# An LSTM scan with a residual: x @ Wx by Strassen products over pairs of steps, one tanh for three gates, and new orders

## The chip, the cores and the metric

One core of a Trainium2 chip. The metric is device time in microseconds of one execution. The kernel before took 2259.08 us, the median of three runs (2258.97 to 2259.52).

## The reference

Input x has 16 sequences of 512 steps with 512 features; h0 is 16 x 512, Wx and Wh are 512 x 2048, b has 2048 entries. All are float32.

```python
xW = jnp.einsum('ntd,dg->ntg', x, Wx) + b
def step(carry, xw_t):
    prev_h, prev_c = carry
    a = xw_t + prev_h @ Wh
    i = sigmoid(a[:, :H]); f = sigmoid(a[:, H:2*H])
    o = sigmoid(a[:, 2*H:3*H]); g = tanh(a[:, 3*H:])
    next_c = f * prev_c + i * g
    next_h = o * tanh(next_c)
    return (next_h, next_c), next_h
_, hs = scan(step, (h0, zeros), swapaxes(xW, 0, 1))
out = x + swapaxes(hs, 0, 1)
```

Each step needs the h of the one before, so h @ Wh and the gates form a chain of 512 links. x @ Wx does not depend on h and can be done at any time ahead.

## The kernel before, in words

**Layout.** A step has only 16 rows. TensorE's array is used as four column groups: matmuls with 32 stationary columns and j = 0..3 write to partitions 32j of one PSUM bank, four of them side by side. 32 columns are 16 rows of two steps (a pair, for x) or 16 rows of two parts of a number (for h). The 512 hidden units lie as 4 (chunk c) x 4 (j) x 32 (u). The hidden units fall into halves a and b (h = 0, 1: chunks 0, 1 and chunks 2, 3); each half has its own PSUM banks `gates[h]`, two for even and odd steps.

**h @ Wh in 16 bits.** Wh is split once into three float16 matrices wq[0..2], and each step's h into float16 parts: p1 (the leading part), p2 (the rest against a stored multiple of h, `hist`) and p2r (a reflected rest by way of `rem`). `products(t, i, kh, h)` (L237) adds one combination: matrix i, rows from half kh, result half h; it is eight matmuls of 256 columns, in four column groups. Matrix 3 needs p1 alone, matrix 1 needs p2 too, matrix 2 needs p2r. In half b, matrix 3 and matrix 2 read a second copy of p1 in another slot, in half a matrix 2 does. The copy is made by ScalarE (L340).

**A step** t is emitted as the list STEP_PE for TensorE, and STEP for VectorE (DVE) and ScalarE (ACT); every engine takes its own instructions strictly in the order in which they are emitted, waiting on semaphores. STEP_PE is twelve products, named by matrix and halves (q3aa: matrix 3, from a to a), then x0 and x1: two chunks of x @ Wx for a pair two ahead (`project`, L214, float32, 512 columns; a float32 matmul runs as two instructions, so x0 and x1 are 16 rows of the trace). The result lands in one of four PSUM banks xb, which already hold the bias (`put_bias`, L198, ACT).

STEP turns finished gates into the next h, for a and b interleaved:

- turn and turno (L272, DVE): transposes from PSUM, of g, i, f (192 columns) and of o (64);
- fold and foldo (L279, DVE): join high and low parts, in float32;
- tanh, sig, sigo (L306, L308, L312, ACT): tanh of g, sigmoid of i and f, sigmoid of o; scale (L314, ACT): o times a power of two;
- mix (L316, DVE): i g and f c in one product; cell (L322, DVE): their sum, the new c; ctanh (L324, ACT);
- p1 (L336, DVE), h (L330, DVE, writes `hist`), copy (L340, ACT), p2 (L342), rem (L346), p2r (L350), all DVE.

After STEP come the two seeds of step t + 2 (L224, ACT: they copy x @ Wx of the step from xb into the gate banks, masked by step parity), and in alternate steps either the bias of a coming pair and a residual, or the scaling of a finished pair back to h (`unscale`, L361, ACT) and the transpose of a coming x (`turn_x`, L210, DVE). A residual transposes the scaled pair (hb, L387, DVE), adds x (L388, GpSimd) and stores it: blocks of 16 steps by 32 DMAs (L368), in the last block pair by pair, 8 DMAs each (L377), all on the queue of SyncE (SP). x comes in blocks of 16 steps on the same queue (L177), two blocks ahead, issued in the first step of a block. The last two rows are stored by `last_sum` (L403), partly from ACT's queue.

The start (L538 to L562) scales and splits Wh, does h0 @ Wh (`first_products`, L249), the first x blocks and step 0, in an order written out by hand (START).

Of the kernel before, what the change touches and what calls it, by code (L numbers as in the profile page):

```python
# [22 lines left out]
STEP_PE = "q3aa q3ab q1ab q1aa q2aa q3ba q1ba q2ba q2bb q1bb q2ab q3bb x0 x1"  # L23
STEP = (
    "turn_a turno_a fold_a tanh_a foldo_a sig_a turn_b sigo_a scale_a mix_a fold_b "
    "tanh_b cell_a ctanh_a turno_b foldo_b sig_b p1_a sigo_b h_a copy_a mix_b p2_a "
    "scale_b cell_b rem_a ctanh_b p2r_a p1_b h_b copy_b p2_b rem_b p2r_b"
# [3 lines left out]
    "turn_a turno_a fold_a turn_b foldo_a tanh_a fold_b sig_a turno_b sigo_a foldo_b "  # L31
    "tanh_b mix_a sig_b cell_a sigo_b ctanh_a mix_b cell_b ctanh_b h_a h_b"
)

# [8 lines left out]
    "d2.2 fold_b tanh_a foldo_a sig_a foldo_b r2.6 d3.2 tanh_b sigo_a sigo_b sig_b "  # L46
    "P.1.3 q3.2.s mix_a mix_b P.2.0 cell_a cell_b r2.5 scale_a ctanh_a ctanh_b scale_b "
    "P.2.1 seed.1.0 seed.1.1 p1_a h_a h_b copy_a p1_b q3.5.s p2_a rem_a rem_b p2r_a "
    "q3.6.v copy_b p2_b p2r_b seed.2.0 seed.2.1"
# [4 lines left out]
def lstm_residual(ctx: ExitStack, tc: tile.TileContext, x, h0, wx, wh, b, out):  # L54
# [82 lines left out]
    sc = const.tile([P, 2, 4], FP, tag="sc", name="sc")  # L137
    neg = const.tile([P, P], FP, tag="neg", name="neg")
    neg16 = const.tile([P, P], HP, tag="neg16", name="neg16")
    rows = [const.tile([P, P], FP, tag=f"rows{h}", name=f"rows{h}") for h in range(2)]  # L140
    S, RS, RS2, RSL = ([sc[:, h, i : i + 1] for h in range(2)] for i in range(4))
# [5 lines left out]
    AT = (((1, 3, 0), (0, 3, 1)), ((0, 3, 2), (0, 2, 3)))  # L147
    SLOTS = (((1, 2, 3, 4), (1, 0, 4, 3)), ((0, 1, 3, 4), (1, 0, 3, 2)))
# [3 lines left out]
        [const.tile([P, 2, 5 * N], HP, tag=f"parts{h}{i}", name=f"parts{h}{i}") for i in range(2)]  # L152
# [42 lines left out]
    xT = {}  # L195
# [4 lines left out]
    def turn_x(q):  # L200
        s, i = divmod(q, XP)
        if i == 0 or q <= FIRST:

            a, e = (i, i + 1 if q < FIRST else XP)
            seen = tmp.tile([P, XP, NK], FP, tag="seen", name=f"seen_{q}")
            nc.vector.tensor_copy(
                seen[:, a:e], xs[s].rearrange("p i (c u) -> p i c u", c=NK)[:, a:e, :, 0]
            )
        xT[q] = xtp.tile([P, NK, Q], FP, tag="xT", name=f"xT_{q}")
        nc.vector.transpose(xT[q].rearrange("p c m -> p (c m)"), xs[s][:, i])  # L210

    def project(q, c):
        for j in range(NJ):
            nc.tensor.matmul(  # L214
                xb[q % NXB][j * Q : (j + 1) * Q],
                lhsT=xT[q][:, c],
                rhs=wx_j[:, c, j],
                start=False,
                stop=False,
                skip_group_check=True,  # L220
            )

    def seed(t, h):
        nc.scalar.mul(  # L224
            gates[h][t % 2][:, :GU].rearrange("p (g u) -> p g u", g=G),
            xb[t // 2 % NXB].rearrange("p (g h u) -> p h g u", g=G, h=2)[:, h],
            mask[:, t % 2 : t % 2 + 1],
        )


    def products(t, i, kh, h):
        g = gates[h][t % 2]
        a = parts[kh][t % 2]
        k = AT[kh][t % 2][i - 1]
        for cc in range(2):
            for j in range(NJ):
                nc.tensor.matmul(  # L237
                    g[j * Q : (j + 1) * Q, :GU],
                    lhsT=a[:, cc, k * N : (k + 2) * N],
                    rhs=wq_j[i - 1][:, 2 * kh + cc, h, j],  # L240
                    start=False,
                    stop=False,
                    skip_group_check=True,
                )

    def first_products(c):
        for e in range(2):
            for j in range(NJ):
                nc.tensor.matmul(  # L249
                    xb[0][j * Q : (j + 1) * Q, (1 - e) * GU : (2 - e) * GU],  # L250
                    lhsT=hT0[:, c],
                    rhs=wh_j[:, c, e, j],
                    start=False,
                    stop=False,
                    skip_group_check=True,
                )


    gc = [state.tile([P, 2, 2 * N], FP, tag=f"gc{h}", name=f"gc{h}_init") for h in range(2)]
# [28 lines left out]
    def slots(t, h, kind):  # L288

        k = SLOTS[h][(t + 1) % 2][kind]  # L290
        return parts[h][(t + 1) % 2][:, :, k * N : (k + 1) * N]
# [4 lines left out]
    def act(t, op, h):  # L296
# [8 lines left out]
        elif op == "tanh":  # L305
            nc.scalar.activation(gc[h][:, 0], v["pre", h][:, 0], AF.Tanh)  # L306
        elif op == "sig":
            nc.scalar.activation(  # L308
                new("sif", t, h, [P, 2, 2 * N]), v["pre", h][:, 1:3], AF.Sigmoid
            )  # L310
# [4 lines left out]
        elif op == "mix":  # L315
            nc.vector.tensor_tensor(  # L316
                new("pr", t, h, [P, 2, 2 * N]), v["sif", h], gc[h], ALU.mult
            )
        elif op == "cell":
            gc[h] = state.tile([P, 2, 2 * N], FP, tag=f"gc{h}", name=f"gc{h}_{t}")  # L320
            pr = v["pr", h]
            nc.vector.tensor_tensor(gc[h][:, 1], pr[:, 0], pr[:, 1], ALU.add)  # L322
        elif op == "ctanh":
            nc.scalar.activation(new("tch", t, h, [P, 2 * N]), gc[h][:, 1], AF.Tanh)  # L324
# [10 lines left out]
        elif op == "p1":  # L335
            nc.vector.tensor_tensor(  # L336
                slots(t, h, 0), two(v["os", h]), two(v["tch", h]), ALU.mult
            )
        elif op == "copy":
            nc.scalar.copy(slots(t, h, 2), slots(t, h, 0))  # L340
        elif op == "p2":
            nc.vector.scalar_tensor_tensor(  # L342
                slots(t, h, 1), slots(t, h, 0), -LO, hl(t, h), ALU.mult, ALU.add
            )
        elif op == "rem":
            nc.vector.scalar_tensor_tensor(  # L346
                new("rem", t, h, [P, 2, N]), slots(t, h, 0), -LO, hl(t, h), ALU.mult, ALU.add
            )
        else:
            nc.vector.scalar_tensor_tensor(  # L350
                slots(t, h, 3), v["rem", h], 2.0, slots(t, h, 1), ALU.mult, ALU.subtract
            )
# [4 lines left out]
    def unscale(p, h):  # L357
        if h == 0:
            hs[p] = work.tile([P, NK, Q], FP, tag="hs", name=f"hs_{p}")
        a = slice(2 * h, 2 * h + 2)  # L360
        nc.scalar.mul(hs[p][:, a], hist[p // XP][:, p % XP, a], RSL[h])  # L361
# [20 lines left out]
    def residual(p):  # L382
# [3 lines left out]
        hb = work.tile([P, P], FP, tag="hb", name=f"hb_{p}")  # L386
        nc.vector.transpose(hb, hs[p].rearrange("p c m -> p (c m)"))  # L387
        nc.gpsimd.tensor_tensor(ob[s][:, i], hb, xs[s][:, i], ALU.add)  # L388
        if s == NS - 1:
            put_pair(s, i)  # L390
        elif i == XP - 1:
# [18 lines left out]
    hT0 = work.tile([P, NK, Q], FP, tag="hT0", name="hT0", bufs=1)  # L410
    warm = const.tile([1, 1], FP, tag="warm", name="warm")
    brow = const.tile([1, G * H], FP, tag="brow", name="brow")
    ones = const.tile([1, Q], FP, tag="ones", name="ones")
    nc.scalar.dma_start(out=brow, in_=b.rearrange("(o f) -> o f", o=1))
# [7 lines left out]
    nc.vector.memset(ones, 1.0)  # L422
    nc.gpsimd.memset(neg, 0.0)
# [45 lines left out]
    for bank in xb:  # L469
        for e in range(2):  # L470
            for j in range(NJ):
                nc.tensor.matmul(  # L472
                    bank[j * Q : (j + 1) * Q, (1 - e) * GU : (2 - e) * GU],
                    lhsT=ones,
                    rhs=brow.rearrange("p (e g c j u) -> p e j g c u", e=2, g=2, c=NK, j=NJ)[
                        :, e, j
                    ],
# [23 lines left out]
    def scales(h):  # L501
# [15 lines left out]
        nc.vector.tensor_scalar(rows[h], neg, RS[h], -1.0, ALU.mult, ALU.mult)  # L517
# [11 lines left out]
    def split(op, n, on_act):  # L529

        c, e = divmod(n, 2)
        w = wh_sb[:, c, e * GH : (e + 1) * GH]
        f = [q[:, c, (1 - e) * GH : (2 - e) * GH] for q in wq]
        if op[0] == "d":
            i = int(op[1])
            for m in range(2):
# [3 lines left out]
                    lhsT=rows[c // 2] if i == 1 else neg16,  # L540
# [8 lines left out]
        elif op == "q2" and n in BY_PE:  # L549
            nc.vector.scalar_tensor_tensor(f[1], w, RS[c // 2], f[0], ALU.mult, ALU.subtract)  # L550
        elif op == "q1":
            cast(on_act, f[0], w, RS2[c // 2])
        elif op == "r1":
            r1[n] = tmp.tile([P, GH], FP, tag="r1", name=f"r1_{n}", bufs=4)
            nc.vector.scalar_tensor_tensor(
                r1[n], w, RS[c // 2], f[0], ALU.mult, ALU.subtract
# [9 lines left out]
    def start(op, a="", b=""):  # L566
# [4 lines left out]
        elif op == "hT":  # L571
            nc.vector.transpose(hT0.rearrange("p c m -> p (c m)"), h_in)
        elif op == "xT":
# [17 lines left out]

    for t in range(1, T):
        s, ti = divmod(t, XB)
        q, half = divmod(t + 4, 2)
        if ti == 0:
            hist[s] = outp.tile([P, XP, NK, Q], FP, tag="hist", name=f"hist_{s}")

        for op in STEP_PE.split():
            if op[0] == "x":
                if q < NP:  # L600
                    project(q, 2 * half + int(op[1:]))
            else:
                products(t, int(op[1]), "ab".index(op[2]), "ab".index(op[3]))
# [4 lines left out]

        if t == T - 3:
            for h in range(2):  # L610
                unscale(t // 2, h)
            residual(t // 2)
        if t + 2 < T:
            seed(t + 2, 0)
        if t == T - 2:
# [5 lines left out]
        elif t % 2 == 0:  # L621
            if q + 1 < NP:
                put_bias(q + 1)
            residual(t // 2 - 1)
        elif t < T - 3:
            for h in range(2):
                unscale(t // 2, h)
            if q + 1 < NP:
                turn_x(q + 1)
        if t + 2 < T:  # L630
            seed(t + 2, 1)
        if ti == 0 and s + 2 < NS:
# [29 lines left out]
```

## Time and profile before

| | |
|---|---|
| median of the runs shown | 2259.08 us |
| span of the profiled execution | 2257.4 us |
| median less span | 1.7 us |
| granted TensorE clock, mean | 0.999 |
| products, start to start, steps 3 to 508 | 4.337 us a step |
| last products (step 511) start | 2248.18 us |
| last DMA issue starts | 2254.6 us |

The profiled execution's own device time is not listed apart from its span; its span is set beside the median. How to read it: the share of busy time is a mean over the run, but from about 45 us to 2235 us the run is one step repeated, so the timeline of a few steps says all about it. A timeline row gives start, duration, engine, line and operation, the tile written and those read, and in brackets the idle time before it with what released it. Neighbouring instructions of one kind are merged, and the end of a group of matmuls is modelled; starts are the better numbers. PE is TensorE's matmuls, PEld its weight loads, which can run ahead. Times within a step, in what follows, count from the start of its first x matmul where nothing else is said.

### The profile page before, as it was taken

How to read it: one execution, taken by the hardware profiler on the slowest of the kernel's cores; microseconds unless marked ns; L12 is line 12 of the kernel's file. 1: busy time of each engine (PE TensorE's matmuls, PEld its weight loads, DVE VectorE, ACT ScalarE, POOL GpSimd, SP SyncE). 2: the span in 40 equal slices, each digit the busy share in tenths (PEclk: the TensorE clock that was granted, in tenths of full speed). 3: DMA queues.
4: the chain of work that ended last, by engine and by line, in shares of the span. 5: the costliest groups of instructions: out<-in, count | busy, mean ns of one | idle time of the engine just before them, and what ended most of it. 6: DMA issues, size and time to landing. Idle time of an engine off the chain costs nothing.

```text
span 2257.4 us, 137977 instructions
## 1 busy us (share of the span) xinstructions
PE 2245.5 (99%) x57412; PEld 1506.4 (67%) x57412; DVE 1951.0 (86%) x11859; ACT 1834.0 (81%) x7958; POOL 132.8 (6%) x291
## 2 busy tenths in 40 slices
PE   9999999999999999999999999999999999999998
PEld 4666666666666666666666666666666666666665
DVE  7888888888888888888888888888888888888888
ACT  7888888888888888888888888888888888888887
POOL 2000000000000000000000000000000000000000
PEclk9999999999999999999999999999999999999999
DMA  5111111111111111101111111111111111111001
GB/s 166 20 21 23 21 16 17 18 23 23 17 17 16 23 22 19 17 16 20 23 22 15 17 18 23 22 17 17 16 22 23 19 17 17 20 22 22 14 9 17
DMA packets 297844, 50.94 MB, mean 23 GB/s; under 512 B 294721, under 2 KB 295169, under 8 KB 297217
## 3 DMA queue, kind: packets, MB, share of 16 engines
q1 hardware_dynamic: 296160, 41.86, 11.5%
q8 instruction: 450, 7.37, 1.4%
q14 instruction: 176, 1.44, 0.2%
q0 software_dynamic: 896, 0.23, 0.0%
q10 hardware_dynamic: 162, 0.02, 0.0%
HBM read 25.21 MB, written 16.78 MB: 19 GB/s over the span
## 4 chain that ended last, share of the span: by engine, by line
PE 99%; DVE 0%; issue 0%; ACT 0%; DVEq 0%
PE gates L237 59%; PE xb L214 39%; PE gates L538 1%; PE xb L472 0%; PE xb L249 0%; PE gates L461 0%; DVE gt L272 0%; DVE preo L279 0%; DVE pre L279 0%; DVE gc L322 0%; DVE gto L272 0%; DVE pr L316 0%; DVE parts L336 0%; DVE hb_last L397 0%; DVE last_o L399 0%
## 5 line engine op out<-in xcount | busy, mean ns | idle before, releaser
L237 PEld LDWEIGHTS <-parts 128*32 128x32 f16 x49056 | 1256.8, 96 | 405.9 <-DVE parts L336 301.7
L237 PE MATMUL gates<-wq,parts 128*32 128x256 f16 x49056 | 1427.8, 273 | 4.2 <-DVE parts L336 4.2
L214 PE MATMUL xb<-wx_sb,xT 128*32 128x512 f32 x8192 | 967.0, 592 | 0.0
L272 DVE STREAM_TRANSPOSE gt<-gates 128x192 f32<-128x192 f32 x1024 | 392.4, 383 | 216.2 <-PE gates L237 167.1
L214 PEld LDWEIGHTS xb<-wx_sb,xT 128*32 128x32 f32 x8192 | 239.4, 110 | 321.1 <-issue 318.1
L224 ACT ACTIVATE gates<-xb,mask 128x256 f32<-128x256 f32 x1024 | 450.8, 441 | 0.9 <-PE xb L214 0.9
L306 ACT ACTIVATE gc<-pre 128x32 f32<-128x32 f32 x1022 | 234.6, 230 | 259.4 <-DVE pre L279 247.5
L314 ACT ACTIVATE os<-so,sc 128x32 f32<-128x32 f32 x1022 | 329.2, 322 | 16.6
L340 ACT COPY parts<-parts 128x32 f16<-128x32 f16 x1022 | 214.8, 210 | 131.7 <-DVE parts L336 131.7
L279 DVE SCALAR_TENSOR_TENSOR pre<-gt 128x96 f32<-128x96 f32 x1024 | 254.4, 248 | 0.0
L308 ACT ACTIVATE sif<-pre 128x64 f32<-128x64 f32 x1024 | 244.9, 239 | 0.0
L388 POOL TENSOR_TENSOR ob<-hb,xs 128x128 f32<-128x128 f32 x255 | 116.5, 457 | 2107.2 <-DVE hb L387 2025.0
L272 DVE STREAM_TRANSPOSE gto<-gates 128x64 f32<-128x64 f32 x1024 | 230.6, 225 | 0.0
L324 ACT ACTIVATE tch<-gc 128x32 f32<-128x32 f32 x1024 | 226.7, 222 | 0.5
L312 ACT ACTIVATE so<-preo 128x32 f32<-128x32 f32 x1024 | 226.8, 222 | 0.3 <-DVE preo L279 0.3
L350 DVE SCALAR_TENSOR_TENSOR parts<-rem,parts 128x32 f16<-128x32 f32 x1022 | 196.3, 192 | 35.5
L279 DVE SCALAR_TENSOR_TENSOR preo<-gto 128x32 f32<-128x32 f32 x1024 | 192.7, 188 | 17.5
L342 DVE SCALAR_TENSOR_TENSOR parts<-parts,hist 128x32 f16<-128x32 f16 x1022 | 192.2, 188 | 17.7
L316 DVE TENSOR_TENSOR pr<-sif,gc 128x64 f32<-128x64 f32 x1022 | 205.1, 201 | 0.1
L336 DVE TENSOR_TENSOR parts<-os,tch 128x32 f16<-128x32 f32 x1022 | 196.9, 193 | 0.0
L322 DVE TENSOR_TENSOR gc<-pr 128x32 f32<-128x32 f32 x1024 | 192.6, 188 | 0.1
L330 DVE SCALAR_TENSOR_TENSOR hist<-os,tch 128x32 f32<-128x32 f32 x1022 | 188.8, 185 | 0.0
(67 smaller groups left out, 750.7 us busy)
## 6 DMA issues: line engine op xcount, KB each, us to landing
xs<-in_x_dram SPq DMA_DIRECT2D x992, 16.0 KB, 2.0
out_dram<-ob SPq DMA_DIRECT2D x992, 16.0 KB, 1.6
wh_sb<-in_L_cond_Wh_dram SPq DMA_DIRECT2D x8, 512.0 KB, 7.8
wx_sb<-in_L_cond_Wx_dram SPq DMA_DIRECT2D x8, 512.0 KB, 12.6
out_dram<-ob SPq DMA_DIRECT2D x56, 8.0 KB, 1.5
xs<-in_x_dram SPq DMA_DIRECT2D x40, 8.0 KB, 2.3
xs<-in_x_dram POOLq DMA_DIRECT2D x24, 8.0 KB, 5.4
out_dram<-last_o SPq DMA_DIRECT2D x6, 8.0 KB, 1.5
```

The source lines that it names most:

```text
L214: nc.tensor.matmul(xb[q % NXB][j * Q : (j + 1) * Q], lhsT=xT[q][:, c], rhs=wx_j[:, c, j], start=False, stop=False, skip_group_check=True,)
L224: nc.scalar.mul(gates[h][t % 2][:, :GU].rearrange("p (g u) -> p g u", g=G), xb[t // 2 % NXB].rearrange("p (g h u) -> p h g u", g=G, h=2)[: ...
L237: nc.tensor.matmul(g[j * Q : (j + 1) * Q, :GU], lhsT=a[:, cc, k * N : (k + 2) * N], rhs=wq_j[i - 1][:, 2 * kh + cc, h, j], start=False, st ...
L272: nc.vector.transpose(gt.rearrange("p b m -> p (b m)"), gates[h][t % 2][:, b0 * Q : b1 * Q])
L279: nc.vector.scalar_tensor_tensor(pre.rearrange("p g (c n) -> p (g c) n", c=2), gt[:, :, (1 - t % 2) * N : (2 - t % 2) * N], 1.0 / LO, gt[: ...
L306: nc.scalar.activation(gc[h][:, 0], v["pre", h][:, 0], AF.Tanh)
L308: nc.scalar.activation(new("sif", t, h, [P, 2, 2 * N]), v["pre", h][:, 1:3], AF.Sigmoid)
L312: nc.scalar.activation(new("so", t, h, [P, 2 * N]), v["preo", h][:, 0], AF.Sigmoid)
L314: nc.scalar.mul(new("os", t, h, [P, 2 * N]), v["so", h], S[h])
L316: nc.vector.tensor_tensor(new("pr", t, h, [P, 2, 2 * N]), v["sif", h], gc[h], ALU.mult)
L324: nc.scalar.activation(new("tch", t, h, [P, 2 * N]), gc[h][:, 1], AF.Tanh)
L340: nc.scalar.copy(slots(t, h, 2), slots(t, h, 0))
```

## The change

Four things.

1. **Strassen.** From the seventh pair of pairs (M0 = 6) on, x @ Wx is not done pair by pair (2 chunks a step, each 512 columns) but for two pairs (four steps) at once. The block matrix has two pairs by two halves of the features on the left and two halves of the features by two halves of the gates on the right; seven products of blocks (each two chunks, 256 columns) replace eight. Over four steps 14 units are put on TensorE, three and a half a step (PHASES: "5:1l" is the left half of a unit's columns, 128). The sums of weights are built once on DVE and ACT during steps 1 to 16 (`sum_w`), into Wh's freed storage. Sums of x (128x64, `sum_x`), a wider transpose (`turn_set`, 128x256) and two additions in PSUM (`add_side`, 128x256) are new work of DVE; `copy_first`, `copy_side` and two biases of 256 columns (for two of 512) new work of ACT.
2. **One tanh.** For i and f the split weights, the bias and the x and h0 read are halved, so that their pre-activations arrive halved: sigmoid(a) = (1 + tanh(a/2)) / 2. One ACT instruction of 96 columns (act) takes the place of tanh and sig. mix becomes (t + 1) * (g, c), cell p0 + 0.5 p1, both scalar_tensor_tensor; c is kept doubled, ctanh scales by 0.5.
3. **p1 written twice** by one DVE instruction (64 columns, inputs read twice), so ACT's copy is gone, and both halves use the same slots.
4. **Orders.** New STEP_PE, STEP, LAST and START. Products are also issued by half ("q2ab." and "q2ab," are its two chunks). Both seeds stand right after STEP. unscale and residual treat two pairs at once, every four steps. Blocks of x are loaded in the fourth step of a block.

The diff, cut:

```diff
-STEP_PE = "q3aa q3ab q1ab q1aa q2aa q3ba q1ba q2ba q2bb q1bb q2ab q3bb x0 x1"
+STEP_PE = "q3aa q3ab q1aa q1ab q2aa q3ba q2ab. q1ba q2ba q2bb. q2ab, q3bb q2bb, q1bb"
 STEP = (
-    "turn_a turno_a fold_a tanh_a foldo_a sig_a turn_b sigo_a scale_a mix_a fold_b "
-    "tanh_b cell_a ctanh_a turno_b foldo_b sig_b p1_a sigo_b h_a copy_a mix_b p2_a "
-    "scale_b cell_b rem_a ctanh_b p2r_a p1_b h_b copy_b p2_b rem_b p2r_b"
+    "turn_a turno_a fold_a act_a foldo_a sigo_a turn_b scale_a mix_a turno_b cell_a ctanh_a "
+    "fold_b act_b foldo_b sigo_b p1_a scale_b h_a mix_b p2_a cell_b ctanh_b rem_a p2r_a "
+    "p1_b h_b rem_b p2_b p2r_b"
 )
...
+M0 = 6
+PHASES = (
+    "1:0 1:1 5:0 5:1l",
+    "5:1r 6:0 6:1 2:0",
+    "2:1 7:0 7:1 3:0l",
+    "3:0r 3:1 4:0 4:1",
+)
...
+        nc.vector.tensor_scalar(xH[q], xT[q], 0.5, None, ALU.mult)
...
+    def turn_set(m):
+        s, i = divmod(2 * m, XP)
+        arrived(2 * m)
+        XT[m] = xtp.tile([P, 2, NK, Q], FP, tag="XT", name=f"XT_{m}")
+        XS[m] = xtp.tile([P, 4, 2, Q], FP, tag="XS", name=f"XS_{m}", bufs=2)
+        nc.vector.transpose(
+            XT[m].rearrange("p a c m -> p (a c m)"),
+            xs[s][:, i : i + 2].rearrange("p i f -> p (i f)"),
+        )
...
+    def strassen(m, k, i, part):
+        w = right(k, i).rearrange("p (g c j u) -> p j g c u", g=2, c=NK, j=NJ)
+        g = {"": slice(0, 2), "l": slice(0, 1), "r": slice(1, 2)}[part]
         for j in range(NJ):
             nc.tensor.matmul(
-                xb[q % NXB][j * Q : (j + 1) * Q],
-                lhsT=xT[q][:, c],
-                rhs=wx_j[:, c, j],
+                region(m, k)[j * Q : (j + 1) * Q, g.start * P : g.stop * P],
+                lhsT=left(m, k, i),
+                rhs=w[:, j, g],
...
+    def copy_first(m):
+        nc.scalar.copy(region(m, 2), region(m, 1))
+
+    def add_side(m, k):
+        nc.vector.tensor_tensor(region(m, k), region(m, 1), side[m], ALU.add)
+
+    def copy_side(m):
+        side[m] = work.tile([P, GU], FP, tag="side", name=f"side_{m}")
+        nc.scalar.copy(side[m], region(m, 5))
...
+        elif op == "act":
+            nc.scalar.activation(gc[h][:, 0:3], v["pre", h], AF.Tanh)
...
+            nc.vector.scalar_tensor_tensor(
+                new("pr", t, h, [P, 2, 2 * N]), gc[h][:, 1:3], 1.0, gc[h][:, ::3], ALU.add, ALU.mult
             )
...
+            nc.scalar.activation(new("tch", t, h, [P, 2 * N]), gc[h][:, 3], AF.Tanh, scale=0.5)
...
+            twice = [
+                two(v[n, h]).rearrange("p c (r n) -> p c r n", r=1).to_broadcast([P, 2, 2, N])
+                for n in ("os", "tch")
+            ]
+            k = 3 - t % 2
             nc.vector.tensor_tensor(
-                slots(t, h, 0), two(v["os", h]), two(v["tch", h]), ALU.mult
+                parts[h][(t + 1) % 2][:, :, 1 : k + 2 : k], twice[0], twice[1], ALU.mult
             )
-        elif op == "copy":
-            nc.scalar.copy(slots(t, h, 2), slots(t, h, 0))
...
+        if t % 4 == 0 and M0 <= (t + 4) // 4 < NM:
+            copy_side((t + 4) // 4)
+        if t + 2 < T:
+            for h in range(2):
+                seed(t + 2, h)
...
+        if t <= 16:
+            sum_w(2 * t - 2)
+            sum_w(2 * t - 1)
+        r = t % 4
+        if r == 3:
+            if M0 <= (t + 5) // 4 < NM:
+                copy_first((t + 5) // 4)
+            if M0 <= (t + 9) // 4 < NM:
+                turn_set((t + 9) // 4)
+                sum_x((t + 9) // 4, 5)
+            if t + 1 < T - 3:
+                unscale(t // 2 - 1, 2, 0)
+        elif r == 0:
+            if M0 <= (t + 4) // 4 < NM:
+                add_side((t + 4) // 4, 3)
+            if M0 <= (t + 8) // 4 < NM:
+                sum_x((t + 8) // 4, 7)
+            if t > 0:
+                unscale(t // 2 - 2, 2, 1)
+            if t == T - 4:
+                residual(t // 2 - 2, 2)
+        elif r == 1:
+            if M0 <= (t + 3) // 4 < NM:
+                add_side((t + 3) // 4, 8)
+            if M0 <= (t + 7) // 4 < NM:
+                sum_x((t + 7) // 4, 6)
+                bias_main((t + 7) // 4)
+        else:
+            if M0 <= (t + 6) // 4 < NM:
+                sum_x((t + 6) // 4, 3)
+                bias_side((t + 6) // 4)
+            if 4 < t < T - 4:
+                residual(t // 2 - 3, 2)
+        if ti == 3 and s + 2 < NS:
             load_xs(s + 2)
```

## The prediction

> **What bounds the kernel now.** I read the page's first part, then the chain of work that ended last, then the timeline of one step in the middle, then the timeline of the last steps, which have no x @ Wx left. The page:
>
> ```profile
> span 2257.4 us, 137977 instructions
> PE 2245.5 (99%) x57412; PEld 1506.4 (67%) x57412; DVE 1951.0 (86%) x11859; ACT 1834.0 (81%) x7958; POOL 132.8 (6%) x291
> ...
> PE 99%; DVE 0%; issue 0%; ACT 0%; DVEq 0%
> ```
>
> TensorE is busy all the time and the chain never leaves it. So less matmul work should shorten the run, but only until something else is late. The timeline of step t (start, duration, engine, line) tells how soon that is:
>
> ```profile
> 1003.32 2.67 PEld L237 LDWEIGHTS <-parts 128*32 128x32 f16 x96 [0.58 <-DVE parts L336]
> ...
> 1003.47 2.79 PE L237 MATMUL gates<-wq,parts 128*32 128x256 f16 x96
> ...
> 1005.45 0.38 DVE L272 STREAM_TRANSPOSE gt<-gates 128x192 f32<-128x192 f32 x1 [0.35 <-PE gates L237]
> ...
> 1006.09 1.89 PE L214 MATMUL xb<-wx_sb,xT 128*32 128x512 f32 x16
> ...
> 1006.32 0.38 DVE L272 STREAM_TRANSPOSE gt<-gates 128x192 f32<-128x192 f32 x1
> ...
> 1006.62 0.18 DVE L316 TENSOR_TENSOR pr<-sif,gc 128x64 f32<-128x64 f32 x1
> ...
> 1006.91 0.18 DVE L322 TENSOR_TENSOR gc<-pr 128x32 f32<-128x32 f32 x1
> ...
> 1007.16 0.21 ACT L324 ACTIVATE tch<-gc 128x32 f32<-128x32 f32 x1
> ...
> 1007.41 0.19 DVE L336 TENSOR_TENSOR parts<-os,tch 128x32 f16<-128x32 f32 x1
> ...
> 1007.81 2.79 PE L237 MATMUL gates<-wq,parts 128*32 128x256 f16 x96
> ```
>
> The products of a step start at 1003.47, its x matmuls at 1006.09, the next products at 1007.81: 2.62 + 1.72 = 4.34 us. (Products of step 3 start at 45.07, those of step 508 at 2235.40: 4.337 us a step over 505 steps.) While TensorE does x, the chain runs: turn_b (L272) at 0.23 after the x matmuls begin, mix_a 0.30 later, cell_a 0.29, ctanh_a 0.25, p1_a 0.25. Weights can load 0.24 after p1_a starts, 1007.65, and x ends at 1007.81. **The chain has 0.16 us to spare, no more.** The last steps confirm it:
>
> ```profile
> 2239.34 0.19 DVE L336 TENSOR_TENSOR parts<-os,tch 128x32 f16<-128x32 f32 x1
> ...
> 2239.58 2.91 PE L237 MATMUL gates<-wq,parts 128*32 128x256 f16 x96 [1.39 <-DVE parts L336]
> ...
> 2240.51 0.22 ACT L340 COPY parts<-parts 128x32 f16<-128x32 f16 x1 [0.26 <-DVE parts L336]
> ...
> 2240.78 1.43 PEld L237 LDWEIGHTS <-parts 128*32 128x32 f16 x56 [0.19 <-ACT parts L340]
> ...
> 2242.55 0.38 DVE L272 STREAM_TRANSPOSE gt<-gates 128x192 f32<-128x192 f32 x1
> ...
> 2243.89 2.91 PE L237 MATMUL gates<-wq,parts 128*32 128x256 f16 x96 [1.39 <-DVE parts L336]
> ```
>
> With no x matmul at all a step still takes 2243.89 - 2239.58 = 4.31 us (the next 4.29; I use 4.30). Removing x work alone is therefore worth 0.04 us a step; the other edits of the change decide what it yields. The reader sees why the chain is so long here: weights wait for the ACT copy of p1_b (L340), and turn_b starts 2.97 after the products instead of 2.62 + 0.23 = 2.85.
>
> **The change, part by part.** Strassen runs from step 19 to 506 (step 19 still does an old block besides).
>
> TensorE. Per four steps 28 passes of 256 columns take the place of 16 of 512: 7 for 4 in each step. A 512 pass takes 1.72 / 4 = 0.43. A 256-column float32 pass stands in h0 @ Wh (L249, at 18.84): 16 matmuls, four passes, in 1.07. The last one's own length is about 0.38 (a 512 one has 0.59 for 0.43, so 0.165 more than its pass) and a start without preloaded weights costs about 0.04 (L214 at 23.73: two passes in 1.06), so (1.07 - 0.38 - 0.04) / 3 = 0.217. Seven make 1.52. Of them two are cut into halves of 128 columns, shorter than the 0.12 that four weight loads take (PEld L214 x4): I add 0.02. x phase 1.54, step 2.62 + 1.54 = **4.16**. Bounds: 1.50 (0.43 / 2 each) to 1.72 (nothing gained).
>
> One page speaks against short passes. The trace's row first: the 96 products of 256 columns, 24 groups of four, take 2.62, 0.109 a group, while a float32 pass of 512 takes 0.43, four times 0.1075; short instructions cost 1 to 2 ns more than their share. The Trainium skill, "TensorEngine Tiling (Array Packing)", Instruction Overhead, says: "Each matmul has ~60 cycle overhead on TRN2". Read as added time, at the warm clock of 2.4 GHz in "TensorE: Matmul & The Clock Gate", What's actually happening, three more passes a step would be an estimated 0.075 us, and the sum some 37 us higher; the row does not bear that out.
>
> Chain. It loses three things. The ACT copy goes: p1 writes both places, so q3ba waits for p1_b alone, 0.23 earlier (L340's length and a signal); turn_b comes at 2.85. One tanh of 96 columns replaces tanh and sigmoid: 0.25 by the rows of 32 (0.230) and 64 (0.239); mix_a would be ready at about 0.47 after x starts, but DVE is in turn_b until 0.53, as before, so this gains nothing itself and only pays for turn_a's 0.1 (three and a half units of products now follow gates a, not four). Between mix_a and cell_a stands turno_b (0.13) instead of fold_b (0.17): 0.25 instead of 0.29. ctanh_a no longer stands behind tanh_b on ACT: 0.24. p1 with 64 columns takes about 0.02 more (bounds 0 and 0.05). From products to products: 2.85 + 0.30 + 0.25 + 0.24 + 0.25 + 0.26 = **4.15**. Both limits meet, which makes 4.16 the likely step; the b side is close too (p2r_b at about 2.89 after x starts, wanted by q2ba at 3.17 less 0.25).
>
> DVE tail. After p2r_b DVE has from 3.00 to about 3.63 until turn_a of the next step. Into it go, in turn: XT transpose 128x256 plus a sum (0.30 for 128 columns and 0.16 for 128 more by L272's slope; 0.46 + 0.03 + 0.14 = 0.64); an addition in PSUM (0.42 by L399's 0.29 and L562's 1.21; 0.35 until the next issue) plus a sum, 0.49, twice; a sum plus hb 128x256, 0.52. These fit, just. Queued behind are turn_a and with it everything; if PSUM or the width costs 0.1 more, the step is late by nearly that. The additions wait for ACT's copy of the side block, at about 2.55, and for x matmuls over by 1.54: both earlier than 3.0. Bounds per step: 0 to 0.15.
>
> ACT (81%) loses two copies (0.21) and two sigmoids (0.24) a step and gains about 0.4 in some steps: from ctanh_b at 1.95 to the next act_a at 4.3 it has 2.3, needs at most 1.7. The POOL sum of twice the width (0.46 to 0.9) has four steps. SP's loads, now at step 3 of a block behind the stores, have 20 steps. All three at nothing; if ACT's cover were gone it would be late by what it lacks, at most 0.2.
>
> So 487 x (4.337 - 4.16) = **-86.2**.
>
> Start. DVE gets four halvings of 128x128 (0.28 each), two small scales and a rows operation; ACT and the matmuls cover part: +1.2 (0 to 2). Steps 1 to 16 also sum weights: per step two DVE operations of 256 columns, 0.35 each by L550's 1.28 for 1024, odd steps with xT and its half as well, even ones up to 8 with a wait for ACT (two seeds, bias 0.58, scaling 0.4). With the old x phase of 1.72 turn_a may start at 4.03 after x without loss. Odd steps end at 3.00 + 0.33 + 0.20 + 0.70 = 4.23 to 4.25: 8 x 0.22, and once 0.65 for the first XT. Steps 2, 4 and 8 wait for ACT until 3.95 and end at 4.30: 3 x 0.27; step 6 has hb too, 0.65; steps 10 and 14 some 0.05 each. Together 4.0. Step 17 has 0.2, step 19 the second x phase, 1.5. +5.7 (2 to 9).
>
> End. SP issues the stores:
>
> ```profile
> 2209.66 41.91 SPq L377 DMA_DIRECT2D out_dram<-ob  x56
> 2251.67 3.31 SPq L403 DMA_DIRECT2D out_dram<-last_o  x6
> ```
>
> The last eight of L377 start at 2246.67, L403 at 2251.67: 0.62 each, and even now SP is done with the backlog only as the last rows come ready (2254.17). After the change pairs are stored by two, from step 506: 16 + 16 + 8 + 4 + 2 = 46 issues. They begin 2.7 after products 507 start (before: hb at 1.3, POOL until 2.2; wider 0.5 more), so the span ends at 2.7 + 45 x 0.62 + 2.8 (last issue, landing, end: 2254.6 to 2257.4) = 33.4, against 2257.4 - 2231.06 = 26.3. **+7.1** (0 to 8).
>
> Sum: 2257.4 - 86.2 + 1.2 + 5.7 + 7.1 = 2185.2. The profiled execution's span lies 1.7 below the median of 2259.08; with that, **2187**.
>
> **Rivals.**
> 1. The DVE tail overruns and turn_a is late by 0.08 on the mean: step 4.24, 487 x 0.097 = 47, time 2226. For it: tails of 0.64 and 0.52 in 0.63, in order. Against: four rows are cheap enough. 0.14.
> 2. Slower: a 256-column pass costs nearly a 512 one's share of fixed time, so that the x phase stays 1.72. Then the step is 4.34 and start and end remain: 2259.1 + 14 = 2273. It decides from 0.241 a pass (1.69; 14 / 487 = 0.029 gained). Against: L249's 0.217 and the products' 0.109. 0.06.
> 3. Better: pass at half of 0.43, step 4.14, and start and end mostly hidden (+3): 2259.1 - 96 + 3 = 2166. Against: SP's 0.62 is a plain row. 0.12.
> That the change does not do what it says is excluded for the count of matmuls; the halves in 16-bit products leave their number at 96.
>
> **How the numbers follow.** Forecast (step 4.14 to 4.19, 2172 to 2202): 0.66; rivals 0.14, 0.06, 0.12; 0.02 for no change. A measurement here tells 0.2% (4.5 us) from no change. Faster 0.66 + 0.14 + 0.12 = 0.92, same 0.02, slower 0.06. The range reaches from a little under rival 3 to rival 1: 2162 to 2228.
>
> **What would show it.** Products to products near 4.16 and x phase near 1.54 in the middle; PEld waiting for p1_a with TensorE's gap under 0.03; turn_a released by PE, not late behind DVE; no wait for ACT's copies; first twenty steps about 6 late; SP the last in the chain, with L403's successor some 7 us after the last transposes. Wrong would be: turn_a released by DVE itself, a pass over 0.23, or an end without SP's backlog.

## The result and the profile after

The changed kernel takes 2227.43 us (median, 2226.84 to 2228.06) against 2259.3 (2258.97 to 2259.8): ratio 0.986, 95% interval 0.9846 to 0.9874, so 32 us faster, where the prediction said 72. The first part of its page and its chain:

```profile
span 2225.2 us, 152487 instructions
PE 2187.3 (98%) x65604; PEld 1658.1 (75%) x65604; DVE 2113.4 (95%) x12392; ACT 1573.2 (71%) x5910; POOL 109.6 (5%) x164
...
PE 29%; DVE 23%; issue 21%; SPq 21%; DMA 4%; POOL 2%; ACT 1%; DVEq 0%; POOLq 0%
```

The chain no longer stays on TensorE: VectorE, SyncE's transfers and even GpSimd, 5% busy, stand in it. SyncE's share is no limit of this size, though: the profile puts the wait of one small copy (`seen`, below) down to the output stores, and the chain then follows the stores. With that copy gone from VectorE (run 4) SyncE has 3% and "issue" 2%. The starts of the products (timeline of TensorE in the middle of the run) show where:

```profile
1003.70 2.81 PE L343 MATMUL gates<-wq,parts 128*32 128x256 f16 x96
1007.86 2.81 PE L343 MATMUL gates<-wq,parts 128*32 128x256 f16 x96
1012.25 2.80 PE L343 MATMUL gates<-wq,parts 128*32 128x256 f16 x96
...
1029.12 2.81 PE L343 MATMUL gates<-wq,parts 128*32 128x256 f16 x96
1033.66 2.81 PE L343 MATMUL gates<-wq,parts 128*32 128x256 f16 x96 [0.23 <-DVE parts L444]
```

Most steps (334 of 487) take about 4.16 (the first two lines), the forecast. One of four takes 4.39 (1007.86 to 1012.25), and one of sixteen 4.54 (1029.12 to 1033.66; two of these 30 take 4.9, why is open). The mean over the 487 steps from products 20 to products 507 is 4.243.

Against before, in the two profiled executions (spans 2257.4 and 2225.2; "S20" is the start of step 20's products):

| stretch | before | after | difference | forecast |
|---|---|---|---|---|
| to S1 | 36.4 | 37.2 | +0.8 | +1.2 |
| S1 to S20 | 82.4 | 92.7 | +10.2 | +5.7 |
| S20 to S507 | 487 x 4.337 | 487 x 4.243 | -46.0 | -86.2 |
| S507 to the end | 26.3 | 29.1 | +2.8 | +7.1 |

The slow step of four is the one behind the tail with the residual (t % 4 = 2). The timeline of all engines there:

```profile
1009.96 0.38 DVE L378 STREAM_TRANSPOSE gt<-gates 128x192 f32<-128x192 f32 x1
1010.02 0.73 POOL L497 TENSOR_TENSOR ob<-hb,xs 128x256 f32<-128x256 f32 x1 [16.14 <-DVE hb L494]
...
1010.40 0.47 DVE L385 SCALAR_TENSOR_TENSOR pre<-gt 128x96 f32<-128x96 f32 x1
...
1010.90 0.28 ACT L411 ACTIVATE gc<-pre 128x96 f32<-128x96 f32 x1 [1.37 <-DVE pre L385]
```

turn_a starts 2.10 after the products (1007.86 to 1009.96), exactly as in the step before (1003.70 to 1005.80): the tail is not late. But fold_a, elsewhere 0.24, takes 0.47, and ends 0.12 after GpSimd's addition (1010.87, 1010.75). The activation and all of the chain are 0.23 late from there.

The slow step of sixteen has another cause, the copy `seen` with which VectorE looks at a newly loaded block of x:

```profile
1030.51 0.19 DVE L456 SCALAR_TENSOR_TENSOR parts<-rem,parts 128x32 f16<-128x32 f32 x1
...
1030.88 0.20 DVE L214 COPY seen<-xs 128x32 f32<-128x32 f32 x1 [0.18 <-DMA out_dram<-ob]
1030.99 0.44 DVE L243 STREAM_TRANSPOSE XT<-xs 128x256 f32<-128x256 f32 x1
...
1031.61 0.38 DVE L378 STREAM_TRANSPOSE gt<-gates 128x192 f32<-128x192 f32 x1
```

The program lets it wait for eight DMA semaphores. The loads were done long ago (SyncE issued the last at 983), yet XT starts 0.48 after p2r_b in place of 0.11, and turn_a is late by as much: 2.49 after the products. The stores named in the bracket are not what it waits for. Before the change the same copy also started 0.37 after p2r_b, and there the profile names no transfer; none had landed on its semaphores for 8 us:

```profile
987.33 0.19 DVE L350 SCALAR_TENSOR_TENSOR parts<-rem,parts 128x32 f16<-128x32 f32 x1
...
987.70 0.19 DVE L206 COPY seen<-xs 128x32 f32<-128x32 f32 x1 [0.18 <-issue]
```

What stands between p2r_b and the copy are four instructions of VectorE's sequencer, which look at the semaphores (minimum, median and longest in ns; first and last start; the copy of 1030.88):

```profile
L214 DVEq EVENT_SEMAPHORE  x4: 21/50/50, 1030.5 to 1030.8; - x4
```

Before the change the tail usually ended 0.35 ahead of turn_a (the idle time in the prediction's row at 1005.45); turn_a still came 1.98 after the products in the step of 987.70, as at 1005.45, and 483 of 487 steps took 4.3: the copy cost nothing.

### The profile page after: what moved, and what is told of

Same layout as the page of the kernel before. It is cut to its first block, busy times and chain, and to the rows that moved or that the text cites. A ratio compares the mean times of both kernels' runs of the same rounds, so it can differ in the third digit from the quotient of the medians.

```text
span 2225.2 us, 152487 instructions
## 1 busy us (share of the span) xinstructions
PE 2187.3 (98%) x65604; PEld 1658.1 (75%) x65604; DVE 2113.4 (95%) x12392; ACT 1573.2 (71%) x5910; POOL 109.6 (5%) x164
## 4 chain that ended last, share of the span: by engine, by line
PE 29%; DVE 23%; issue 21%; SPq 21%; DMA 4%; POOL 2%; ACT 1%; DVEq 0%; POOLq 0%
PE gates L343 21%; SPq L475 18%; PE xb L278 8%; DVE gt L378 5%; DMA out_dram<-ob 3%; SPq L184 3%; DVE pre L385 2%; DVE parts L444 2%; DVE gto L378 2%; POOL ob L497 2%; DVE pr L417 2%; DVE parts L456 1%; DVE hb L494 1%; DVE preo L385 1%; DVE rem L452 1%
## 5 line engine op out<-in xcount | busy, mean ns | idle before, releaser
L343 PEld LDWEIGHTS <-parts 128*32 128x32 f16 x49056 | 1166.5, 96 | 290.4 <-DVE parts L444 152.7
L411 ACT ACTIVATE gc<-pre 128x96 f32<-128x96 f32 x1022 | 289.6, 283 | 534.6 <-DVE pre L385 534.6
L278 PE MATMUL xb<-sums,XS 128*32 128x256 f32 (+1 forms) x6832 | 380.2, 349 | 0.0
L278 PEld LDWEIGHTS xb<-sums,XS 128*32 128x32 f32 x6832 | 201.5, 110 | 116.7
L278 PE MATMUL xb<-wx_sb,XT 128*32 128x256 f32 x3904 | 274.0, 379 | 0.0
L444 DVE TENSOR_TENSOR parts<-os,tch 128x64 f16<-128x64 f32 x1022 | 230.8, 226 | 12.6
L417 DVE SCALAR_TENSOR_TENSOR pr<-gc 128x64 f32<-128x64 f32 x1022 | 213.7, 209 | 0.0
L452 DVE SCALAR_TENSOR_TENSOR rem<-parts,hist 128x32 f32<-128x32 f16 x1022 | 192.3, 188 | 17.7
L497 POOL TENSOR_TENSOR ob<-hb,xs 128x256 f32<-128x256 f32 x128 | 93.1, 727 | 2096.3 <-DVE hb L494 1738.8
L423 DVE SCALAR_TENSOR_TENSOR gc<-pr 128x32 f32<-128x32 f32 x1024 | 174.9, 171 | 0.1
```

The costliest lines, as they stand in the source:

```text
L278: nc.tensor.matmul(region(m, k)[j * Q : (j + 1) * Q, g.start * P : g.stop * P], lhsT=left(m, k, i), rhs=w[:, j, g], start=False, stop=Fals ...
L343: nc.tensor.matmul(g[j * Q : (j + 1) * Q, :GU], lhsT=parts[kh][t % 2][:, cc, k : k + 2].rearrange("p k n -> p (k n)"), rhs=wq_j[i - 1][:, ...
L411: nc.scalar.activation(gc[h][:, 0:3], v["pre", h], AF.Tanh)
L417: nc.vector.scalar_tensor_tensor(new("pr", t, h, [P, 2, 2 * N]), gc[h][:, 1:3], 1.0, gc[h][:, ::3], ALU.add, ALU.mult)
L444: nc.vector.tensor_tensor(parts[h][(t + 1) % 2][:, :, 1 : k + 2 : k], twice[0], twice[1], ALU.mult)
```

## Experiments

Theory A: GpSimd's wider addition holds up fold_a (122 x 0.23 = 28 us) and the arrival of x costs 30 x 0.37 = 11; what the prediction said of TensorE and of the chain holds. Theory B, near the prediction's first rival: VectorE's tail is too long by itself. Time "now" is 2227.4.

**1. The addition nearly taken away.** The output buffers are constant tiles here, and the edit is cut to the addition.

```
-        nc.gpsimd.tensor_tensor(ob[s][:, i : i + n], hb, xs[s][:, i : i + n], ALU.add)
+        w = slice(0, 1)
+        nc.gpsimd.tensor_tensor(ob[s][:, i : i + n, w], hb[:, :, w], xs[s][:, i : i + n, w], ALU.add)
```

> The changed kernel, but GpSimd's residual addition takes one column of each 128 (2 elements for 256 on each partition), so that most of the output holds zeros in place of h + x; VectorE's transpose of h before it (128x256) stays, as do all stores. Theory A (the addition holds up VectorE's fold_a, whose row grows from 0.24 to 0.47 beside it): every fourth step falls from 4.39 to 4.16, 122 x 0.23 = 28 us, time 2199. Theory B (the tail after p2r_b is too long by itself: a 128x256 transpose and a sum in front of turn_a): the transpose is still there, so the step stays at 4.39 and the time at 2227.

Measured 2200.2: A's number. The mean step falls from 4.243 to 4.189, worth 26.3, with the transpose still in place. The groups by line, of the kernel before, of the changed kernel and of this one, show which instruction it was (busy us, then mean ns):

```profile
L279 DVE SCALAR_TENSOR_TENSOR pre<-gt 128x96 f32<-128x96 f32 x1024 | 254.4, 248 | 0.0
```

```profile
L385 DVE SCALAR_TENSOR_TENSOR pre<-gt 128x96 f32<-128x96 f32 x1024 | 279.1, 273 | 0.0
```

```profile
L386 DVE SCALAR_TENSOR_TENSOR pre<-gt 128x96 f32<-128x96 f32 x1024 | 249.2, 243 | 0.0
```

30 ns over 1024 folds are 30 us of VectorE, about the 27 us gained. B is out for these steps.

**2. The addition twice.**

```
+        for k in range(2):
             nc.gpsimd.tensor_tensor(ob[s][:, i : i + n], hb, xs[s][:, i : i + n], ALU.add)
```

> The changed kernel with GpSimd's residual addition issued twice, one after the other, with the same operands and the same result. Theory A (a GpSimd addition blocks VectorE instructions with two SBUF inputs for as long as it runs): the second one, another 0.73 us, meets the output gate's fold, mix_a and cell_a; every fourth step grows by 0.5 to 0.7, time 2288 to 2312. Theory B (length of VectorE's tail): GpSimd is 5% busy and VectorE gets no instruction more, time 2227.

Measured 2255.1, +27.6: an idle engine's extra work costs time, which B excludes, but less than half of what I wrote. The timeline says why:

```profile
1003.69 1.55 POOL L498 TENSOR_TENSOR ob<-hb,xs 128x256 f32<-128x256 f32 x2 [15.55 <-DVE hb L494]
...
1004.07 0.47 DVE L385 SCALAR_TENSOR_TENSOR pre<-gt 128x96 f32<-128x96 f32 x1
1004.46 0.18 DVE L385 SCALAR_TENSOR_TENSOR preo<-gto 128x32 f32<-128x32 f32 x1
1004.56 0.37 DVE L378 STREAM_TRANSPOSE gt<-gates 128x192 f32<-128x192 f32 x1
...
1004.89 0.43 DVE L417 SCALAR_TENSOR_TENSOR pr<-gc 128x64 f32<-128x64 f32 x1
```

fold_a is held to the end of the first addition, the small fold slips through between the two, and turn_b, which reads PSUM, runs beside the second one unharmed (0.37). Only mix_a meets it: 0.43 for 0.18. The step grows by 0.21, from 4.39 to 4.59. Held are the instructions with two inputs in SBUF; a transpose is not. This fits the Trainium skill, "SBUF — State Buffer", Who interferes with whom: a VectorE instruction with two SBUF inputs contends with a GpSimd instruction that reads SBUF, and the one that comes second is blocked until the first is done. The rows (0.24 to 0.47, 0.18 to 0.43) agree.

**3. The addition moved** to where VectorE has no such instruction: single pairs, first in the tails of t % 4 = 0 and 1, and the sums for products 7, 6, 3 together at t % 4 = 2.

```
+        if r < 2 and 7 < t < T - 6:
+            residual(t // 2 - 4 + r, 1)
...
-            if 4 < t < T - 4:
-                residual(t // 2 - 3, 2)
+            if t == T - 6:
+                residual(t // 2 - 3, 2)
```

> The changed kernel with the residual by single pairs again: transpose and addition of 128x128 first in the tails of steps with t % 4 = 0 and 1, in front of the addition in PSUM; the sums of x for products 7, 6 and 3 all go to the tail of t % 4 = 2. Instruction count on VectorE rises by one transpose in four steps. Theory A: GpSimd's 0.46 runs beside the addition in PSUM and turn_a, which have at most one SBUF input, so fold_a is free; all steps but one in 16 take 4.16, time 2199. Theory B (length of the tail alone): the tails of t % 4 = 0 and 1 grow to 0.30 + 0.35 = 0.65 and more against 0.63 of room, so two steps in four are late by 0.02 to 0.15 and one gains 0.23: time 2205 to 2236.

```profile
1005.92 0.40 DVE L297 TENSOR_TENSOR xb<-xb,side 128x256 f32<-128x256 f32 x1
1006.08 0.46 POOL L499 TENSOR_TENSOR ob<-hb,xs 128x128 f32<-128x128 f32 x1 [12.05 <-DVE hb L495]
1006.29 0.38 DVE L378 STREAM_TRANSPOSE gt<-gates 128x192 f32<-128x192 f32 x1
...
1006.73 0.24 DVE L385 SCALAR_TENSOR_TENSOR pre<-gt 128x96 f32<-128x96 f32 x1
```

The fold has its 0.24 again and the mean step is 4.188, as without the addition. The time is 2207.3 and not 2199, which by itself would fit B's 2205 to 2236; but B had two steps of four late, and none is: all but those behind `seen` take about 4.16. The rest lies at the end: from S507 to the end it takes 37.0 for 29.1. The last pairs of the last but one block are added three steps later, so its stores begin 18.4 before S507 instead of 30.8, and SyncE, busy from there to the end, is the last.

**4. The arrival waited for on ScalarE**, which copies each set of x.

```
-        arrived(2 * m)
...
+        passed[m] = xtp.tile([P, 2, P], FP, tag="XC", name=f"XC_{m}", bufs=1)
+        nc.scalar.copy(passed[m], xs[s][:, i : i + 2])
```

> The changed kernel, but once Strassen runs VectorE no longer looks at the arrival of a block of x: ScalarE copies each set of x (128x256) one step ahead, waits there for the loads, and VectorE transposes the copy. Theory A (VectorE's wait for eight DMA lanes and the small copy behind it put 0.37 on one step in 16): 30 x 0.37 = 11 us go, time 2216. Rival: the wait is only where VectorE happens to stand, and the step is late for the transpose and the sum behind it: time 2227. If ScalarE has no room for 0.35 more in four steps, or is held by the same wait, the time is above 2227.

Measured 2217.1, -10.3: A. No step of 4.54 or 4.9 is left between S20 and S507, while 122 of 4.4 are; ScalarE had room for the copies (0.41 each).

**5. Without Strassen** (`M0 = 128`, no sums of Wx).

> The changed kernel without Strassen: all steps do x @ Wx in the plain blocks (as its steps 1 to 18 do), no sums of Wx are made; one tanh, p1 written twice, and the new orders stay. If the prediction is right that TensorE's 4.34 bounds such a step and that the other edits alone are worth nothing, the step is 4.34, the time 2258 to 2268 (4.337 a step as before, up to 0.04 more in every fourth for the held fold_a, start +1, end +3). Rival: the other edits shorten the step themselves, below 2250.

Measured 2268.3, ratio 1.0039 (1.0024 to 1.0054): the other edits alone are worth nothing and cost 9. The step is 4.348, behind the residual as elsewhere: its x phase, 32 matmuls of 256 columns for 16 of 512, takes 1.73 for 1.72. The addition of twice the width costs nothing here. With no sum of x in front of it it starts 1.82 after the products (1022.15 after 1020.33; 2.15 in the changed kernel), and is over 0.03 after the fold begins; the fold keeps its 0.24.

**6. Strassen alone**, with what its tails bring (residuals by two pairs, both seeds right after STEP, x loaded in the fourth step of a block) and with tanh in place of sigmoid, but with two activations, p1 and its copy, and the orders of products and STEP as before. First try, with both activations of a half called at one place:

> The changed kernel with Strassen, and with the other edits undone: two activations for g and for i, f, p1 written once and copied by ScalarE, the places in parts, the order of products and the order of a step's other instructions as before the change. The prediction read from the last steps of the kernel before that removing x work alone leaves a step of 4.30: 487 x 0.037 = 18 gained, start +11, end +3, and GpSimd's addition and the arrival of x on top (0 to 39): time 2255 to 2294. Rival: shorter x phases help by themselves, below 2240.

Measured 2364.9, far off: in this version half b's second activation stood in front of ctanh_a, which came 3.95 after the products in place of 3.81. With before's order kept:

> Once more the changed kernel with the products by Strassen and the other edits undone, now with the elementwise order of the kernel before kept exactly: in the run before this one both activations of half b stood in front of ctanh_a, which came 0.14 later for it. Prediction: step 4.30 as in the last steps of the kernel before, 487 x 0.037 = 18 gained, start +11, end +3, GpSimd's addition and the arrival of x up to 39 on top: 2255 to 2294. Rival: the changed products cost this chain more than that (as 2365 would have it): above 2310.

Measured 2291.3. TensorE's timeline:

```profile
1002.35 2.91 PE L343 MATMUL gates<-wq,parts 128*32 128x256 f16 x96
1006.82 2.91 PE L343 MATMUL gates<-wq,parts 128*32 128x256 f16 x96
1011.12 2.92 PE L343 MATMUL gates<-wq,parts 128*32 128x256 f16 x96
```

A step of 4.30 (so are most others), as read blind from the last steps of before, and one of 4.47 where the addition is. The mean is 4.366, so of the 2291 some 30 are GpSimd's addition and the arrival of x. So: before 2259, Strassen alone 2291, the other edits alone 2268, both 2227. Neither part pays by itself; with Strassen the others are worth 64, with the others Strassen is worth 41.

**7. The parts of the chain.** One tanh cut in two:

```
-            nc.scalar.activation(gc[h][:, 0:3], v["pre", h], AF.Tanh)
+            nc.scalar.activation(gc[h][:, 0], v["pre", h][:, 0], AF.Tanh)
+            nc.scalar.activation(gc[h][:, 1:3], v["pre", h][:, 1:3], AF.Tanh)
```

> The changed kernel with the one tanh of 96 columns cut into two instructions (32 and 64 columns), nothing else. If the chain stands within 0.02 of the bound, as in the prediction, mix_a comes 0.13 to 0.16 later in every step: time 2287 to 2309. If TensorE alone bounds the step and the chain has room, under 2232.

Measured 2315.1: most steps take 4.33, +0.17 each, a little above the range. The chain has no room.

p1 written once, with before's places in `parts` and the ScalarE copy:

> The changed kernel with p1 written once, its second place by a ScalarE copy, and the places in parts as before the change, so that TensorE's sixth unit of products (q3ba) waits for the copy of p1_b again. By the prediction's terms turn_b comes 0.12 later (2.97 for 2.85), and the copy is 0.23 later than p1_b: 0.12 to 0.23 in every step, time 2288 to 2344. Rival: p1 of twice the width costs as much as it saves, time within 6 us of 2227.

Measured 2252.1, +25, under my range. The mechanism is there: weights wait for the copy, and turn_b comes 2.96 after the products (2.97 expected, 2.86 now). But most steps take 4.25 or a little more, +0.09, and not the 0.12 to 0.23 that I wrote: the copy's wait does not come on top of the later turn_b. And turn_a comes later too (2.20 after the products for 2.10), so that behind the residual it meets less of GpSimd's addition: fold_a 0.33 there in place of 0.47. These steps fall from 4.39 to 4.32, so what one wait costs, the other partly gives back.

The old order of products:

```
-STEP_PE = "q3aa q3ab q1aa q1ab q2aa q3ba q2ab. q1ba q2ba q2bb. q2ab, q3bb q2bb, q1bb"
+STEP_PE = "q3aa q3ab q1ab q1aa q2aa q3ba q1ba q2ba q2bb q1bb q2ab q3bb"
```

> The changed kernel with the order of the products as before the change (q2ba q2bb before q1bb q2ab, no halves). q2ba, which needs p2r_b, is then wanted 0.11 earlier than in the changed order, where p2r_b is only just in time, and gates a are finished 0.11 earlier. If PE order matters as the prediction's chain has it (turn_a 2.97 to 2.85), TensorE stalls 0.05 to 0.15 in each step for p2r_b: 2250 to 2300. Rival: the earlier end of gates a gives it back: within 10 us of 2227.

Measured 2263.7, +36: step 4.318. Weights wait 0.20 for p2_b in each step, and gates a are no earlier for it (turn_a still 2.10 after the products). The time is in my range, but I had named p2r_b as what would be waited for.

**8. The start.**

```
-        if t <= 16:
-            sum_w(2 * t - 2)
-            sum_w(2 * t - 1)
+        if t <= 32:
+            sum_w(t - 1)
```

> The changed kernel with one operation of the sums of Wx in each of steps 1 to 32 in place of two in each of 1 to 16; Strassen begins 16 steps later (M0 = 10). Steps 1 to 19 now take 10.3 more than at 4.337 each. If two operations of 0.35 overrun the tail and one fits, that falls to 0 to 3, and 16 steps at 4.337 for 4.24 cost 1.5: time 2218 to 2222. If the excess is due to the number of operations wherever they stand, 2227 to 2230.

Measured 2222.6, -4.8, just over my range. S1 to S20 falls from 92.7 to 84.5, against 82.4 before. Of these 8.2, 1.5 are the step with two x phases, which only moves to step 35; it and the sixteen steps given to the plain form take some of the gain back.

**9. All repairs together**, with the last two blocks stored by pairs and half of four pairs issued by GpSimd's queue:

```
-        if s == NS - 1:
+        if s >= NS - 2:
...
+                queue = nc.gpsimd if s == NS - 1 and i in (2, 3, 4, 5) and j % 2 else nc.sync
```

> All repairs together: residual by single pairs in the tails of t % 4 = 0 and 1, arrival of x waited for on ScalarE, sums of Wx one in a step, the last two blocks stored by pairs (four pairs of the last block half by GpSimd's queue). If the four causes are separate: 2227 - 27 (steady steps of the pair version) - 11 (arrival) - 6 (sums) - 0 to 5 (end) = 2178 to 2184. If ScalarE's copies and the fuller tails of t % 4 = 0 and 1 collide, above 2190.

Measured 2183.1 (2182.8 to 2183.5), ratio 0.9662 (0.9648 to 0.9677) to before and 44 us under the changed kernel. Its page:

```profile
span 2181.0 us, 152828 instructions
...
PE 96%; DMA 1%; DVE 1%; SPq 1%; ACT 0%; issue 0%; DVEq 0%
```

TensorE bounds the kernel again: step 4.175, end 27.1. This is within 4 us of the blind forecast, which had assumed that nothing else would be late; but the total agrees better than its terms. The steps gain 79.0 and not 86.2 (16 more are plain), and the first steps and the end cost 2.6 and not 14.0.

## Why the prediction was wrong

- **TensorE's step: right.** Products 2.64 (1003.70 to the x matmuls at 1006.34; forecast 2.62), x phase 1.52 (to 1007.86; forecast 1.54). The second rival (passes not cheaper) is out, and the third's step of 4.14 did not come. The Trainium skill's 60 cycles a matmul ("TensorEngine Tiling (Array Packing)", Instruction Overhead), read as added time, would have made the x phase an estimated 1.62; the measurement decides against that reading.
- **VectorE's tail: right but for `seen`.** The tail with the residual ends as turn_a starts (1009.94 and 1009.96, 2.10 after the products as elsewhere); an addition in PSUM takes 0.43 (0.42).
- **The chain: right.** turn_b at 2.86 (2.85), then mix_a 0.31 (0.30), cell_a 0.26 (0.25), ctanh_a 0.19 (0.24), p1_a 0.26 (0.25), products 0.28 (0.26): 4.16 for 4.15. Runs 6 and 7 show that each of the other edits was needed for it.
- **The step that failed: "All three at nothing", for GpSimd.** "The POOL sum of twice the width (0.46 to 0.9) has four steps" asked when its result is wanted, and not what else cannot run while it runs. It cost 26.3 in these steps (run 1). At 0.46, the old width, it would have been over at 1010.48, 0.08 after the fold's start (that width was not tried at this place); the 0.73 of the double width reaches far into it.
- **An instruction not in the sum:** `seen`, 10.8 by the steps of run 4. I listed VectorE's tail by what the change adds, and left out what was there and had been hidden by the very idle time that the change uses up.
- **Start: under-sized.** +10.2 for +5.7. The second x phase at step 19 was as forecast (that step takes 5.87, 1.53 over 4.34). The sums are the rest, 8.7 for 4.2; run 8, where S1 to S20 keeps 2.1 of them, shows that it is two operations a step that don't fit. The same two omissions stand in the difference of 4.5: GpSimd's addition with 1.1 (S1 to S20 is 91.6 in run 1), and `seen`, which stands in the tails of steps 1, 3 and 11 too, with an estimated 1.1 (three times 0.37). The rest was not taken apart.
- **End: over-sized.** +2.8 for +7.1. SyncE's backlog is the last, as said:

```profile
2165.31 20.73 SPq L475 DMA_DIRECT2D out_dram<-ob  x32
2186.15 33.93 SPq L484 DMA_DIRECT2D out_dram<-ob  x56
2220.18 2.73 SPq L513 DMA_DIRECT2D out_dram<-last_o  x6
```

But it is one backlog from 2165 on: the 46 issues that I let begin 2.7 after S507 (2196.12) begin 0.3 before it (2186.15 and 16 x 0.606), and each takes 0.606, not 0.62.
- **The first rival** named 2226 and a step of 4.24, the numbers that came, but for the wrong reason in the larger part: its late turn_a exists only behind `seen` (0.39 in one step of sixteen); the rest is fold_a, with turn_a on time. That its number came is luck. My test for it ("turn_a released by DVE itself") would have passed these steps as good.

Sum: 26.3 + 10.8 + 3.1 (the remaining 4.166 for 4.16, and rounding) in the steps, +4.5 at the start, -4.3 at the end, -0.4 to S1: the 40 us missing. The errors at the start and at the end nearly cancel.

## What to carry to other kernels

When a change removes the slack of one engine, list again everything that this slack was hiding, old instructions too; what the diff adds is only half of the list. A side engine's work is free only if no instruction of the critical chain needs what it holds while it runs: put its long instructions beside instructions of the chain that it cannot hold, and check the chain's own rows for a spread (a mean of 273 ns for a row of 243).

## What the runs showed of the hardware

- GpSimd's addition of two SBUF tensors (0.73 for 128x256) made VectorE's fold take 0.47 for 0.24 and mix_a 0.43 for 0.18 (run 2), while transposes out of PSUM (0.37, 0.38) and an addition of PSUM and SBUF (0.40 here, 0.43 elsewhere) beside it were not longer. Between two GpSimd instructions a waiting VectorE instruction got through.
- A VectorE instruction with eight DMA semaphores to wait for, all long reached, started 0.37 after the instruction ahead of it, against some 0.11 between others; four sequencer instructions of up to 0.05 stand between. It was so before the change (987.33 to 987.70) and after.
